# A literal engine order for the last attention and its mixture of experts, with both halves' expert tiles in one row

## The chip, the cores and the metric

The kernel runs on one core of one Trainium2 chip. The metric is the time of one execution in microseconds of the device. Times of before and after are medians over several runs. The profile is of one execution of its own.

## The reference

The input x holds 8 sequences of 256 tokens, 128 numbers each (2048 tokens in all); `ctx` is a context of 64 rows of 256 numbers for each sequence. Four levels L0 to L3 follow one another, each an attention to the context and a feed-forward part, added to x behind a gate:

```python
x = x + jnp.tanh(g_xattn[3]) * _L3_xattn_ref(ctx_2048, _layernorm(x, axis=-1), mask_BxS2_ik0, L3_xattn_b)
x = x + jnp.tanh(g_ffn[3]) * _L3_ffn_ref(_layernorm(x, axis=-1), L3_ffn_shared_w1, ...)
```

L3's attention has 8 heads of depth 16: `softmax(Q K^T / 4 + b - 1e30 (1 - mask)) V`, with K and V the two halves of the context. L3's feed-forward part is a mixture of experts:

```python
sw1, sw2 = (_bit_quant(shared_w1), _bit_quant(shared_w2))
shared_out = jax.nn.silu(jnp.einsum('btd,fd->btf', h, sw1)) @ sw2.T
probs = jax.nn.softmax(h @ router_w.T, axis=-1)
top_prob, top_idx = jnp.max(probs, axis=-1), jnp.argmax(probs, axis=-1)
h1 = jax.nn.silu(jnp.einsum('btd,efd->ebtf', h, ew1))
eo = jnp.einsum('ebtf,edf->ebtd', h1, ew2)
gate = jax.nn.one_hot(top_idx, N_EXPERTS) * top_prob[..., None]
return shared_out + jnp.einsum('ebtd,bte->btd', eo, gate)
```

Here `h` is a normalised x, the hidden width is 256, and of eight experts each token uses the most probable one.

## The kernel before, in words

x stays on the chip as 16 tiles of 128 tokens (`NT`), 4 chunks of 4 tiles (`NCH`, `TPC`), two halves of 8 tiles (`HT`). The stages run one after another: `l0`, `l1_xattn`, `l1_ffn`, `l2_xattn`, `l2_ffn`, `l3_xattn`, `l3_ffn`. The program says what each engine does, and a scheduler places the instructions of each engine in an order of its own, from its estimates of cost and the order of the program; `issue_after` (in `behind`) keeps an instruction behind a named one. Buffers come from pools with a fixed number of copies; a new tile waits until the old one's last reader is done. PSUM is eight single banks in both L3 stages.

**Attention, `l3_xattn` (L1760 to L1857).** For each of 16 tiles, `weights(t)` makes one score matmul against all heads and context rows at once (`sc`, 128x512, L1786), adds the mask on DVE (L1794), takes the maximum by head on DVE (`all_max`, L289), subtracts it on POOL (L1797), takes the exponential on ACT (L1798) and the sum on DVE (`row_sum`, L318). `turned(t)` transposes the probabilities on PE (`tp`, L1808) and copies them out on ACT (L1809). For each pair of tiles, `summed(b)` multiplies by the values (`o`, L1815), copies (L1817), transposes back (`po`, L1820), divides by the sums (L1822, L1824) and adds to x (L1831). The loop calls `weights` three tiles ahead. Into it are woven: `turn_weights` in the first ten steps (transposes of the expert weights, L1772, and an ACT copy, L1774); `normed3(c)` for chunks 1 to 3 at steps 0, 4 and 8 (layer norm by `ln_apply`, four DVE operations, and a transpose; chunk 0's stands ahead of the last `experts(3)` of `l2_ffn`); `logits3(c)` for chunks 0 to 2 at steps 4, 8 and 12 (norm by DVE statistics and `norm_act`, that is one DVE operation at L358 and four ACT operations at L360; a copy z to DRAM, a transpose, a matmul with the router weights); `routed3(0)` at step 9 and the gathers of half 0 from step 10.

**Routing, `routed3` (L1931).** From the logits of a half: softmax (L320 to L329), `largest` (L646), `counted` (L514, matmuls that count tokens by expert) and `placed` (L529), some 35 small DVE operations. They give each token a place in tiles that hold one expert's tokens each: 15 tiles a half. `sources` (L597) makes the list of tokens by 16 index matmuls (`dp_idx`, L602) and a cast (L604). `fetched3` gathers the 15 tiles of z by indirect DMAs that POOL issues (`gather`, L610).

**Mixture, `l3_ffn` (L1957).** `tiles(half, aside)` is a row of 15 tiles with four operations on each, one behind another by a step: `turn` (transpose L1972, ACT L1974), `first` (expert matmul, 256 wide, L1979, Silu on ACT L1987), `turn_back` (transposes L1992, DVE copy L1994), `second` (two matmuls L1999, DVE copy L2008; after every fourth tile SP writes four to DRAM, L2011). The expert's number is read by PE's sequencer (`tile_expert`). `aside` puts logits of chunk 3 and routing of half 1 in nine pieces into the row of half 0, and the gathers of half 1 at its step 10. `combine` (L623) gathers a half's results back, 8 gathers, and adds them times the probability to x (L640, DVE). `wide` and `shared` are the shared expert on a chunk (L2029 to L2036), with `add_back_t` (a copy on ACT and DVE in turn, L69 to L75, transposes L285, an addition L277). Order: row of half 0, its combination, dense chunk 0, row of half 1 (half 0's additions at steps 8 and 12), combination of half 1, dense chunks 1 to 3, additions of half 1, output (L2062, SP).

Of the kernel before, what the change touches and what calls it, by code (L numbers as in the profile page):

```python
# [24 lines left out]
P = 128  # L25
# [3 lines left out]
NCH = 4  # L29
# [8 lines left out]
def tile_flamingo(ctx: ExitStack, tc: tile.TileContext, a: dict, out: bass.AP, n_sub: int = 8):  # L38
# [1495 lines left out]
    def l2_ffn():  # L1534
        wqp, wkp, wvp, wop, w1p, w2p = (w2f[:, i] for i in range(6))
        load3()
        with psum(8, 0), tc.tile_pool(name="l2f", bufs=1) as cp, tc.tile_pool(name="l2g", bufs=2) as lp:
# [215 lines left out]
            normed3(0)  # L1753
# [3 lines left out]
    def normed3(c):  # L1757
        s.activation(q3["qT"][c % 2], transposed(layernorm(c)), AF.Copy, scale=0.25)

    def l3_xattn():  # L1760
# [15 lines left out]
        with psum(8, 0), tc.tile_pool(name="l3x", bufs=2) as lp:  # L1776
            madd, kb, qTs = q3["madd"], q3["kb"], q3["qT"]
            pTs, sums = {}, {}

            def weights(t):  # L1780

                b = t // 2
                if t % 2 == 0:
                    sums[b] = mk(small, [P, 2, 8], "rs3")
                sc = bank([P, 8, S2], "sc3")
                pe.matmul(  # L1786
                    sc.rearrange("p h m -> p (h m)"),
                    qTs[(t // TPC) % 2][:, (t % TPC) * P : (t % TPC + 1) * P],
                    kb[:, b].rearrange("p h m -> p (h m)"),
                    start=True,  # L1790
                    stop=True,
                )
                pa = mk(lp, [P, 8, S2], "pa3", bufs=4)
                v.tensor_tensor(pa, sc, under(madd[:, b, :], 8), ALU.add)  # L1794
                m = mk(small, [P, 8], "m3")
                all_max(m, pa)
                q3["sub"] = g.tensor_tensor(pa, pa, over(m, S2), ALU.subtract)  # L1797
                s.activation(pa, pa, AF.Exp)  # L1798
                row_sum(sums[b][:, t % 2, :], pa)
                return pa  # L1800

            def turned(t, pa):
                b = t // 2
                if t % 2 == 0:
                    pTs[b] = mk(lp, [P, 4, S], "pT3")
                tp = bank([P, 4, P], "tp")
                for i in range(4):
                    pe.transpose(tp[:, i, :], pa[:, 2 * i : 2 * i + 2, :].rearrange("p t m -> p (t m)"), ident)  # L1808
                s.copy(pTs[b][:, :, (t % 2) * P : (t % 2 + 1) * P], tp)  # L1809

            def summed(b):
# [4 lines left out]
                oT = mk(lp, [P, S], "oT3")  # L1816
                s.copy(oT, o)  # L1817
                po = bank([P, 2, D], "po3")
                for qt in range(2):
                    pe.transpose(po[:, qt, :], oT[:, qt * P : (qt + 1) * P], ident)  # L1820
# [11 lines left out]

            ahead = 3
            ready = {t: weights(t) for t in range(ahead)}
            for t in range(NT):
                if t % TPC == 0 and t // TPC + 1 < NCH:
                    normed3(t // TPC + 1)
                if t + ahead < NT:
                    ready[t + ahead] = weights(t + ahead)
                turned(t, ready.pop(t))  # L1840
                if t % 2:
                    summed(t // 2)
                if turns:
                    turn_weights(*turns.pop(0))

                if t in (4, 8, 12):
                    logits3(t // 4 - 1)
                elif t == 9:
                    run_all(routed3(0))
                elif t == 10:  # L1850
                    fetches = fetched3(0, 2)
                if t in (10, 11):
                    with behind(q3["sub"]):
                        next(fetches)
                elif t == 12:
                    with behind(q3["sub"]):
                        run_all(fetches)  # L1857
# [50 lines left out]
    def logits3(c):  # L1908

        st = mk(small, [P, TPC, 6], "st")  # L1910
        mv = mk(small, [P, TPC, 2], "mv")
        for k in range(TPC):
            v.bn_stats(st[:, k, :], xs(c)[:, k, :])
            v.bn_aggr(mv[:, k, :], st[:, k, :])
        rstd = mk(small, [P, TPC], "rstd")
        v.tensor_scalar(rstd, mv[:, :, 1], 1.0 + 1e-5, 1e-10, ALU.mult, ALU.add)
        power(rstd, rstd, TPC)
        z = mk(act, [P, TPC, D], "xn")
        norm_act(z, c, mv, rstd)
        half, k2 = divmod(c, 2)  # L1920
        if k2 == 0:
            q3["z", half] = dram.tile([HT * P, D], F32, tag=f"z{half}", name=f"z{half}")
        nc.sync.dma_start(q3["z", half][k2 * CW : (k2 + 1) * CW, :].rearrange("(n p) d -> p n d", p=P), z)
        hT = q3["hT"]
        s.activation(hT[:, c, :], transposed(z), AF.Identity, bias=gb3[:, 1:2], scale=gb3[:, 0:1])
        lg = bank([P, TPC, E], "lg")
        for k in range(TPC):
            pe.matmul(lg[:, k, :], hT[:, c, k * P : (k + 1) * P], rw3, start=True, stop=True)
        s.copy(q3["lg"][:, (c % 2) * TPC : (c % 2 + 1) * TPC, :], lg)

    def routed3(half):  # L1931


        pool = q3["pool"]
        pr = softmax8(q3["lg"])
        yield
        ((m, mask),) = largest(pool, pr, 1)
        w = mk(pool, [P, HT], "w3")
        v.tensor_scalar(w, m, tg[:, 7:8], None, ALU.mult)
        q3["w", half] = w  # L1940
        yield
        cnt = counted(pool, [mask])
        yield
        q3["at", half] = yield from placed(pool, [mask], cnt, q3["consts"])

    def fetched3(half, n=2 * HT):

        at, ge = q3["at", half][0:2]
        idx = sources(q3["pool"], at, ge)
        q3["xr", half] = xr = mk(q3["pool"], [P, idx.shape[1], D], "xr")  # L1950
        for t in range(idx.shape[1]):
            if t and t % n == 0:
                yield
            gather(xr[:, t, :], q3["z", half][:, :], idx[:, t : t + 1])

    def l3_ffn():


        with psum(8, 0), tc.tile_pool(name="l3f", bufs=3) as lp:
            w1T, w2T = q3["wT"]  # L1960
            w1e, w2e = (w.rearrange("p (e i) d -> p e i d", i=2) for w in (w1T, w2T))
            hT = q3["hT"]

            def tiles(half, aside):
                ei, xr = q3["at", half][2], q3["xr", half]
                n_tiles = xr.shape[1]
                yg = dram.tile([n_tiles * P, D], F32, tag=f"y3{half}", name=f"y3{half}")
                xrT, h1s, hTs, es, yr, marks = {}, {}, {}, {}, {}, {}

                def turn(t):  # L1970
                    pt = bank([P, P], "ptr")
                    pe.transpose(pt, xr[:, t, :], ident)  # L1972
                    xrT[t] = mk(lp, [P, P], "xrT")
                    s.activation(xrT[t], pt, AF.Identity, bias=gb3[:, 1:2], scale=gb3[:, 0:1])  # L1974

                def first(t):
                    es[t] = e = tile_expert(ei, t)
                    ph = bank([P, 2 * P], "phr")
                    pe.matmul(  # L1979
                        ph,  # L1980
                        xrT[t],
                        w1e[:, bass.ds(e + 1, 1)].rearrange("p e i d -> p (e i d)"),
                        start=True,
                        stop=True,
                    )
                    h1s[t] = mk(lp, [P, 2, P], "h1r")
                    marks[t] = [s.activation(h1s[t].rearrange("p i f -> p (i f)"), ph, AF.Silu)]  # L1987

                def turn_back(t):
                    pt = bank([P, 2, P], "pth")  # L1990
                    for i in range(2):
                        pe.transpose(pt[:, i, :], h1s[t][:, i, :], ident)  # L1992
                    hTs[t] = mk(lp, [P, 2, P], "h1T", bufs=2)
                    v.tensor_copy(hTs[t], pt)  # L1994

                def second(t):
                    y = bank([P, D], "yr")
                    for i in range(2):
                        pe.matmul(  # L1999
                            y,  # L2000
                            hTs[t][:, i, :],
                            w2e[:, bass.ds(es[t] + 1, 1), i, :].rearrange("p e d -> p (e d)"),
                            start=(i == 0),
                            stop=(i == 1),
                        )
                    if t % 4 == 0:
                        yr[t // 4] = mk(lp, [P, 4, D], "yr", bufs=2)
                    marks[t].append(v.tensor_copy(yr[t // 4][:, t % 4, :], y))  # L2008
                    if t % 4 == 3 or t == n_tiles - 1:
                        o, n = t - t % 4, t % 4 + 1  # L2010
                        nc.sync.dma_start(  # L2011
                            yg[o * P : (o + n) * P, :].rearrange("(n p) d -> p n d", p=P), yr[t // 4][:, 0:n, :]
                        )

                for t in range(-2, n_tiles + 1):
                    for f, d in ((turn, 2), (first, 1), (turn_back, 0), (second, -1)):
                        if 0 <= t + d < n_tiles:
                            f(t + d)
                    for f in aside.get(t, ()):
                        with behind(*marks.get(t - 1, ())):  # L2020
                            f()
                return yg
# [114 lines left out]
```

## Time and profile before

| | |
|---|---|
| median of 11 runs | 1323.03 us (1307.28 to 1331.52) |
| profiled execution | 1318.24 us, span 1316.3 us |
| mean granted TensorE clock | 0.866 |
| busy: PE | 1086.7 us (83%) |
| busy: DVE | 644.5 us (49%) |
| busy: ACT | 437.1 us (33%) |
| busy: POOL | 303.8 us (23%) |

The time of a profiled execution is its span and some 2 us around it. The stages of the end, from the timeline: L3's attention 1110.1 to 1215.6 us, row of half 0 to 1251.9, dense chunk 0 and row of half 1 to 1296.6, the rest to 1316.3. A page of the profile has the busy time of each engine (PE matmul, PEld weight load, DVE vector, ACT scalar, POOL, SP for DMA issue), its share by fortieths of the span, groups of instructions by line, and the timeline of one engine. In a group's row the columns are: line, engine, operation, output and input with their shapes, count; busy time and mean ns of one; idle time of the engine just ahead of them and what ended it. "remote" and "issue" name waits that ended for no reason which the profile shows.

### The profile page before, as it was taken

The numbers are of one execution on the slowest core, as the hardware profiler recorded it, in microseconds if no ns is written. First come the engines' busy times: TensorE is split into PE (matmuls) and PEld (weight loads), VectorE is DVE, ScalarE is ACT, GpSimd is POOL, SyncE is SP. The second block draws the span as 40 slices with busy tenths as digits, with TensorE's granted clock in tenths as the row PEclk, the third lists the DMA queues.
The fourth block names the chain that finished last, engine by engine and source line by source line (L and its number), as shares of the span: only waits on it lengthen the run. The fifth ranks groups of instructions, "written<-read, shape, count | busy, mean of one in ns | idle before, by whom it ended". The sixth has DMA issues, their size and how long they took to land.

```text
span 1316.3 us, 15627 instructions
## 1 busy us (share of the span) xinstructions
PE 1086.7 (83%) x5570; PEld 603.7 (46%) x5570; DVE 644.5 (49%) x1794; ACT 437.1 (33%) x842; POOL 303.8 (23%) x341
## 2 busy tenths in 40 slices
PE   6886697966999999899898987889988898655857
PEld 4554455643444444533455654344443333433734
DVE  4651333543655455443237986257518445653514
ACT  4521242322334433541234444211123333422523
POOL 2157221140100000100102554023133101215152
PEclk9887698975999979787898997988899999765869
DMA  9113110110000003200000002000000000002122
GB/s 246 39 31 53 34 45 22 33 52 8 19 14 7 18 2 98 97 0 0 1 1 1 1 1 59 22 0 1 1 0 0 1 0 0 9 8 38 37 48 79
DMA packets 50811, 37.04 MB, mean 28 GB/s; under 512 B 10280, under 2 KB 46672, under 8 KB 50480
## 3 DMA queue, kind: packets, MB, share of 16 engines
q1 hardware_dynamic: 45488, 26.83, 7.4%
q0 software_dynamic: 3968, 8.13, 3.1%
q10 hardware_dynamic: 1280, 1.09, 0.4%
q8 instruction: 45, 0.74, 0.2%
q14 instruction: 30, 0.25, 0.1%
HBM read 25.34 MB, written 8.13 MB: 25 GB/s over the span
## 4 chain that ended last, share of the span: by engine, by line
PE 65%; DVE 15%; ACT 7%; issue 6%; POOL 4%; another core or an unknown queue 2%; DMA 1%; SPq 1%; DVEq 0%; ACTq 0%; POOLq 0%
PE pymT L1610 4%; PE gur L768 4%; PE st L1038 4%; PE sc L983 4%; PE o L1064 3%; DVE nmx L992 3%; PE pqmT L1610 3%; PE phm L1693 2%; PE pgb L1591 2%; PE pvmT L1610 2%; PE pkmT L1610 2%; PE yr L793 2%; PE yt L1200 2%; PE gu L744 2%
## 5 line engine op out<-in xcount | busy, mean ns | idle before, releaser
L992 DVE TENSOR_REDUCE nmx<-sc 128x2 f32<-128x640 f32 x128 | 97.7, 817 | 80.3 <-PE sc L983 67.0
L221 POOL TENSOR_TENSOR rstd<-rstd,mhalf 128x4 f32<-128x4 f32 (+1 forms) x36 | 34.2, 950 | 383.2 <-DVE rstd L236 317.9
L1047 ACT ACTIVATE pT<-st 128x1024 f32<-128x1024 f32 x64 | 62.1, 1021 | 109.1 <-PE st L1038 109.1
L768 PE MATMUL gur<-arena_a,xrT 128*128 x184 | 70.0, 508 | 0.8 <-issue 0.4
L1610 PE MATMUL pymT<-xe,arena_b 128*128 128x512 f32 x128 | 61.7, 638 | 2.6 <-DVE xe L1602 2.6
L983 PE MATMUL sc<-arena_b 29*128 29x320 f32 x256 | 43.7, 571 | 15.1 <-DVE nmx L992 12.4
L610 POOL DMA_INDIRECT xr<-xk,dp_src x46 | 45.7, 994 | 43.1 <-DVE lg_m L289 29.4
L785 DVE COPY aTr<-pta 128x256 f32<-128x256 f32 x46 | 19.5, 423 | 73.1 <-PE pta L783 43.7
L1464 POOL TENSOR_TENSOR arena_a<-arena_a,rs 128x1024 f32<-128x1024 f32 x16 | 30.4, 1901 | 92.7 <-DVE rs L1463 78.7
L610 POOL DMA_INDIRECT xn<-yg,dp_rows x32 | 30.3, 946 | 75.4 <-DMA yg<-yr 43.1
L1591 PE MATMUL pgb<-gt,e_sel 8*128 8x512 f32 x192 | 40.4, 704 | 7.6 <-ACT gt L1584 7.6
L783 PE MATMUL pta<-ident,sgr 128*128 128x128 f32 x138 | 24.7, 291 | 22.4 <-issue 17.6
L1610 PEld LDWEIGHTS pymT<-xe,arena_b 128*128 128x128 f32 x128 | 25.5, 205 | 38.6 <-issue 23.7
L768 PEld LDWEIGHTS gur<-arena_a,xrT 128*128 128x128 f32 x184 | 35.0, 210 | 17.3 <-issue 7.7
L793 PE MATMUL yr<-arena_a,aTr 128*128 (+1 forms) x276 | 41.7, 292 | 0.0
L983 PE MATMUL sc<-arena_a 29*128 29x320 f32 x256 | 37.2, 492 | 4.1 <-DVE nmx L992 3.8
L610 POOL DMA_INDIRECT xr<-z,dp_src x30 | 28.7, 956 | 44.5 <-DVE dp_ef L318 27.8
L776 ACT ACTIVATE sgr<-gur 128x352 f32<-128x352 f32 x46 | 21.4, 464 | 52.3 <-PE gur L768 35.2
L1443 PE MATMUL sc<-G,t2k 128*128 128x512 f32 x64 | 34.3, 632 | 4.6 <-DVE rs L1462 3.7
L793 PEld LDWEIGHTS yr<-arena_a,aTr 128*128 128x128 f32 (+1 forms) x276 | 37.8, 207 | 0.2
L1038 PE MATMUL st<-arena_b 32*128 32x256 f32 x256 | 36.8, 502 | 1.2 <-DVE nmx L992 1.0
L277 DVE SCALAR_TENSOR_TENSOR x<-yt,tg,x 128x512 f32<-128x512 f32 x16 | 12.0, 748 | 52.2 <-PE yt L1205 29.1
(501 smaller groups left out, 2428.7 us busy)
## 6 DMA issues: line engine op xcount, KB each, us to landing
arena_a<-in_L_ffn_exp_wgu_dram SPq DMA_DIRECT2D x2, 1408.0 KB
yg<-yr SPq DMA_DIRECT2D x10, 256.0 KB
arena_a<-in_L_xattn_Wkv_dram SPq DMA_DIRECT2D x1, 2048.0 KB
y<-yr SPq DMA_DIRECT2D x6, 256.0 KB
x<-in_x_dram SPq DMA_DIRECT2D x4, 256.0 KB
arena_b<-in_ctx_dram ACTq DMA_DIRECT2D x2, 512.0 KB
arena_a<-in_L_ffn_exp_wd_dram SPq DMA_DIRECT2D x2, 512.0 KB
xk<-xk SPq DMA_DIRECT2D x4, 256.0 KB
```

Of the source, the lines that this page charges most:

```text
L221: g.tensor_tensor(dst, src, mhalf[:, 0:n], ALU.pow)
L610: return g.indirect_dma_start(out=dst, out_offset=None, in_=src, in_offset=bass.IndirectOffsetOnAxis(ap=idx, axis=0))
L768: pe.matmul(gu[:, h, 0:352], xrT[t], wgu[:, bass.ds(e + 1, 1), h * 352 : h * 352 + 352].rearrange("p e f -> p (e f)"), start=True, stop=True,)
L793: pe.matmul(y, aT[0:n, i, :], wd[0:n, bass.ds(e + 1, 1), i, :].rearrange("p e d -> p (e d)"), start=(i == 0), stop=(i == 2),)
L983: pe.matmul(scs[j // 2][:, j % 2, 0:K], qp[i : i + 29, k4, t], kp[i : i + 29, k4, b, :], start=True, stop=True,)
L992: l1["max"] = v.tensor_reduce(nmx[qt][:, h0 : h0 + 2], scs[pr][:, :, 0:K], AX.X, ALU.max, negate=True)
L1038: pe.matmul(sts[j // 2][:, j % 2, kt, :], kp[i : i + 32, k4, b, kt * P : (kt + 1) * P], qp[i : i + 32, k4, tb], start=True, stop=True,)
L1047: s.activation(pT[k4, pr], sts[pr], AF.Exp)
L1064: pe.matmul(o[kk][32 * i : 32 * i + n, k, :], w, e, start=(step == 0), stop=(step == 2))
L1443: pe.matmul(sc[:, 8 * k : 8 * k + 8, :].rearrange("p h m -> p (h m)"), xT[:, q], G[:, b, 8 * k : 8 * k + 8, :].rearrange("p h m -> p (h m) ...
L1591: pe.matmul(pg, e_sel4[r, e, :], gt[r], start=True, stop=True)
L1610: pe.matmul(pq, w[:, e, :], xe[:, e, :], start=(e == 0), stop=(e == E - 1))
```

## The change

Both L3 stages run under `manual_schedule` for PE, DVE, ACT and POOL: these engines take their instructions in the order of the program (SP is still scheduled). So the program's own order is written anew.

```diff
-            normed3(0)
+            for c in range(2):
+                for f in normed3(c):
+                    f()
             experts(3)
...
-        with psum(8, 0), tc.tile_pool(name="l3x", bufs=2) as lp:
+        with psum(8, 0), tc.tile_pool(name="l3x", bufs=2) as lp, tc.manual_schedule(engines=all_four):
...
+            beside(3, *normed3(2))
+            beside(7, *normed3(3))
+            for c in range(2):
+                beside(4 * c + 5, *logits3(c))
+            steps = routed3(0)
+            beside(12, *[lambda: next(steps, None)] * 5)
+            beside(13, *logits3(2))
+            scores(0)
+            scores(1)
+            shifted(0)
+            exps(0)
+            for t in range(NT + 1):
+                b = t // 2 - 1
+                if t % 2 == 0 and b >= 0:
+                    outputs(b)
+                if t + 2 < NT:
+                    scores(t + 2)
+                if t + 1 < NT:
+                    shifted(t + 1)
+                if t < NT:
+                    summed(t)
+                    turned(t)
+                if t % 2 == 0 and b >= 0:
+                    added(b)
+                if t + 1 < NT:
+                    exps(t + 1)
                 if turns:
                     turn_weights(*turns.pop(0))
...
+                for f in extra.get(t, ()):
+                    f()
```

`scores`, `shifted` (add, maximum, subtraction), `exps`, `summed` (now the sum by row), `turned`, `outputs` (value matmuls and copy) and `added` (transposes back, division, addition to x) are the pieces of the former `weights`, `turned` and `summed`. `normed3` and `logits3` become three steps each (statistics; normalisation, by `norm_act` in both; transposes and what follows), and `routed3` five, which now also makes the list of tokens; the softmax there takes its maximum from `largest`, and only the largest probability is computed (two DVE operations fewer). `fetched3(half, tiles)` only gathers.

```diff
+            stats, norm, logits = logits3(3)
+            fetched3(0, range(2))
+            stats()
+            h0, h1 = wide(0), wide(1)
+            norm()
+            fetched3(0, range(2, n_tiles))
+            y0 = shared(0, h0)
+            y1 = shared(1, h1)
+            logits()
+            back(0, y0)
+            back(1, y1)
             steps = routed3(1)
...
+            aside = {t: [lambda: next(steps, None)] for t in range(-1, 4)}
+            aside[4] = [lambda: fetched3(1, range(n_tiles))]
+            mid, backs = {}, []
+            aside[n_tiles - 4] = [lambda: mid.update(h=wide(2))]
+            aside[n_tiles - 3] = [lambda: mid.update(y=shared(2, mid["h"]))]
+            aside[n_tiles - 2] = [lambda: back(2, mid["y"])]
+            aside[n_tiles] = [lambda: backs.extend(combined(0))]
+            for i in range(2):
+                aside[2 * n_tiles - 4 + 2 * i] = [lambda i=i: backs[i]()]
+            for t in range(-2, 2 * n_tiles + 1):
+                for f, d in ((turn, 2), (first, 1), (turn_back, 0), (second, -1)):
+                    if 0 <= t + d < 2 * n_tiles:
+                        f(t + d)
+                for f in aside.get(t, ()):
+                    f()
+            h3 = wide(3)
+            tail = combined(1)
+            y3 = shared(3, h3)
+            back(3, y3)
+            for f in tail:
                 f()
```

So all gathers of half 0 are in the mixture, ahead of and beside dense chunks 0 and 1; the 30 tiles of both halves form one row (`n_tiles` is 15), with routing of half 1 in its steps -1 to 3, half 1's gathers at 4, dense chunk 2 at 11 to 13, half 0's combination at 15 and its additions at 26 and 28; dense chunk 3 and half 1's combination follow. `shared` no longer calls `add_back_t`: it copies on ACT always, and `back` does the transposes and the addition.

## The prediction

> **What bounds the kernel now.** The change touches only the L3 stages, so I first read the page's table by fortieths of the span (32.9 us each): PE is busy nine tenths in the middle and falls off at the end.
>
> ```profile
> PE   6886697966999999899898987889988898655857
> PEclk9887698975999979787898997988899999765869
> ```
>
> The last seven slices (from about 1086 us) hold PE at 5 to 8 tenths and the granted clock down to 5 tenths. Next come the windows by stage (columns: start and end, length, busy time of each engine with its instructions, clock, DMA share): the L3 attention in five parts, four parts of the tile row, the tail.
>
> ```profile
> 1109.40:1132.00 22.60, 16.27 (x82) 9.43 (x82) 19.36 (x44) 12.22 (x22) 7.68 (x10) 0.92 0.00 1
> 1132.00:1148.00 16.00, 10.69 (x36) 6.24 (x37) 6.09 (x22) 5.31 (x11) 4.05 (x4) 0.60 0.05 16
> 1148.00:1163.00 15.00, 8.60 (x53) 5.83 (x51) 8.70 (x23) 8.25 (x16) 4.13 (x4) 0.96 0.06 17
> 1163.00:1185.00 22.00, 12.78 (x48) 8.48 (x48) 13.53 (x52) 3.52 (x8) 2.14 (x2) 0.50 0.00 1
> 1185.00:1216.00 31.00, 17.13 (x68) 9.19 (x68) 9.26 (x24) 7.80 (x16) 17.51 (x18) 0.50 0.23 40
> 1216.00:1246.00 30.00, 24.92 (x135) 20.76 (x134) 15.11 (x66) 16.58 (x36) 1.07 (x2) 0.76 0.09 27
> 1257.00:1278.00 21.00, 7.43 (x24) 3.87 (x22) 1.18 (x2) 2.87 (x7) 13.33 (x15) 0.60 0.27 48
> 1278.00:1296.30 18.30, 17.13 (x114) 15.38 (x114) 11.46 (x36) 8.82 (x23) 0.00 (x0) 0.89 0.20 59
> 1296.30:1316.30 20.00, 12.24 (x36) 5.22 (x34) 6.11 (x14) 4.17 (x7) 7.61 (x8) 0.91 0.26 75
> ```
>
> The attention takes 106 us while no engine works more than 65.5 of them (PE), much of that at half clock; DVE works 56.9. It is bound by the order: an engine waits for one whose next instruction is something else. The groups by line show the idle time before each:
>
> ```profile
> L1797 POOL TENSOR_TENSOR pa<-pa,m 128x512 f32<-128x512 f32 x16 | 16.7, 1045 | 47.0 <-ACT pT L1809 15.9 <-DVE dp_gt L543 7.8 <-DVE sm_m L328 7.7
> L1794 DVE TENSOR_TENSOR pa<-sc,arena_a 128x512 f32<-128x512 f32 x16 | 10.9, 687 | 12.1 <-PE sc L1786 12.0
> L1809 ACT COPY pT<-tp 128x512 f32<-128x512 f32 x16 | 9.3, 584 | 35.0 <-PE tp L1808 30.7 <-remote 3.6 <-issue 0.8
> ```
>
> POOL's subtractions wait 15.5 us for routing on DVE and 15.9 for buffers that a late copy holds. The tile row has another loss: in 1257 to 1278 POOL issues gathers without a break and all else stalls. The timeline (start, duration, instruction, idle time before it):
>
> ```profile
> 1269.99 0.42 DVE L1994 COPY h1T<-pth 128x256 f32<-128x256 f32 x1 [11.91 <-remote]
> 1273.55 0.46 ACT L1974 ACTIVATE xrT<-ptr,gb 128x128 f32<-128x128 f32 x1 [6.67 <-issue]
> 1273.64 0.95 POOL L610 DMA_INDIRECT xn<-y,dp_rows  x1 [0.31 <-issue]
> ```
>
> Each hop between engines takes 3 to 12 us here though its producer is done; the Silus of one row step (L1987), 1.21 us apart when undisturbed, are 3.5 and 10.5 apart. The last line is the burst's last gather; from 1278 the row runs again.
>
> **The change, attention.** Work per engine stays nearly the same; each engine gets a literal order, two tiles apart on PE and one on DVE, and routing of half 0 is cut into five steps. DVE's rows: add .687, maximum .679, sum .680 for 16 tiles, 32.7 us; reciprocal .246, multiply .424, add to x .476 for 8 pairs, 9.2; five sets of statistics (chunks 2 and 3 of the queries, 0 to 2 of the mixture) at 2.1, 10.6; routing, some 35 operations of .21 and one of 1.22, 8.5. Sum 61.0. Row durations overlap a little: of about 62 us of rows the windows hold 56.9, so I take 0.92 of 61.0, 56. How tight will DVE be? The nearest pipeline of the same shape in this trace is the L2 attention:
>
> ```profile
> 712.00:784.00 72.00, 66.79 (x311) 42.84 (x309) 64.19 (x155) 33.30 (x71) 39.34 (x41) 1.00 0.00 1
> ```
>
> DVE is busy 89% there (87% with its head), PE at full clock. I take 87%: 64.5 us. The first scores come at 1110.8 (1110.15 before, and .65 of PE for the four transposes of normed3(1), moved into the L2 end; its statistics and normalisation lie beside experts(2)), add 1.1 to the first DVE work, and 6 for what stands alone at the end: the count matmuls' wait (1.2), the last output chain (1), the index matmuls (2 to 3.6) and a cast. Routing runs at steps 12 to 16, so index of half 0 and attention end together: **1182.4**, against 1185.1 for the index before but 1215.6 for the attention. normed3's normalisation goes from DVE to ACT: 4 x .317 of DVE against .163 and 4 x .48 of ACT, which has room (36.7 of 106 us busy). A subtraction on POOL is 1.05 and an Exp .63; with three hops of .1 these 2.0 us fit beside the 2.05 DVE us of a step, so one tile ahead just suffices.
>
> **Mixture, from that index.** (1) Dense chunks 0 and 1 and logits3(3) go ahead of the row: a dense chunk is 1.8 + 1.88 + .66 = 4.4 us of PE (rows of the tail), two of them and .9 of logits 9.7, and some 4.4 of hops: 14.1. Beside it POOL issues half 0's 15 gathers at 1.25 us (.95 and .30), 18.8; they end near 1204 while the row starts at 1196.5 and needs one per 1.21 us, so gathers hide, which before stood alone in 1185 to 1216. (2) The row: 30 x 1.21 = 36.3, and 2.1 to fill; 13 for routing of half 1 inside it (before, half 0's 14 steps beside routing and logits3(3) took 30.1 against 16.9, 13.2 more; half 1 has two DVE operations fewer, but no logits); 4.4 of dense chunk 2; and slow hops. For those the ends are nothing and what bursts cost before: 17 (1257 to 1278, 23 gathers), about 18 (L0, 23 in a row), 7 (L0, 16), 4 to 5 (half 0, 11 in a row), 1.5 (tail, 8). New bursts in the row are 13 (its end: I take 5), 15 (8.5) and 8 (2): 15.5, nearest to the bursts of like length. Row sum 71.3, from 1196.5 to 1267.8. (3) The tail is as before: the last tile's copy ended at 1296.6, the span at 1316.3, 19.7. Writing y, 8 gathers and the last additions are unchanged, and dense chunk 3 (4.4) lies beside the gathers, of which 9.7 us remain if it is late; half 0's combination (8 gathers at step 15, additions at 26 and 28) lies in the row. SP's output writes and y writes keep their order: no y write is queued behind an x that waits. POOL's order is literal as well: 13 gathers stand behind chunk 3's pow, half 0's combination behind 15 gathers, half 1's behind both, each ready before POOL is.
>
> Sum: 1182.4 + 14.1 + 71.3 + 19.7 = **1287.5**, 28.8 less than the span of 1316.3. The profiled execution took 1318.24 (1.9 around its span), 4.8 below the median of 1323.0; the same difference from the median gives **1294**.
>
> **The rivals.** *B, slow hops do not return* (-15.5): nothing but the rows above speaks for a price by burst, and the order of after leaves engines fewer hops to wait for. 1278; with DVE at 95% in the attention another 5.5, 1273. [...]
>
> *C, PE stays at half clock through the attention.* In windows of 4 us the clock fell to .68 behind one with PE 41% busy and to .50 behind one with 20% (1132 to 1136), and stayed at .50 in 1163 to 1216 at 55% busy. At half clock a step of PE costs 4.1 us (scores 1.71, probabilities' transposes .85, weight transposes .85 in ten of the steps, outputs .54 and .22), with logits and queries 76 in all: index at 1111.9 + 76 + 11.6 = 1199.5, 1304.6 in all, **1311**. Against it: at full clock PE needs 2.05 of the 4 us a step that DVE needs, about what held .92 to .96 above. [...]
>
> *D, slower: one tile ahead is too little and the literal order serialises a step.* Then a step is add .69, maximum .68, subtraction 1.05, Exp .63, transposes .85, copy .58 and six hops of .1, 5.1; 16 of them 82, and 20 for statistics and routing that no longer hide, 10 at head and index: index at 1223.5, **1335**. It decides from an index later than 1211 (1316.3 - 105.1), a step of over 4.6 us beside the rest. For it: before, three tiles ahead, a step took 6.6. Against: those steps waited for routing, not for the chain, and L2's attention at two ahead holds DVE at 87%.
>
> *E, no change*: gains are given back in waits for expert weights or buffers, 1323.
>
> **How the numbers follow.** Forecast .50, B .18, C .13, D .15, E .04. The predicted time is the forecast's, 1294. The range reaches from 1268 (B with the tighter DVE, and 5 less of routing in the row) to 1322 (all of C, most of E), leaving out D and a little more. A measurement of this kernel can tell about 0.5%, 6.6 us. Faster by more (under 1316.4): forecast, B and .09 of C, .77; within: the rest of C and most of E, .07; slower: D and a trace of E, .16.
>
> **What would show it.** In the profile after: DVE at 85% or more from the first score to the last index, which comes near 1182; POOL's subtractions no longer waiting for DVE's routing; half 0's gathers beside dense chunks; a row of 30 tiles at 1.21 us with gaps beside gather bursts of 8 to 15 us in all; a tail of 19 to 20. A granted clock of .5 in the attention would be C, steps over 4.6 us D, a row without gaps B. The prediction is wrong altogether if the stages before L3 move, since it takes them as unchanged.

## The result, and the profile after

The changed kernel takes 1300.46 us (median of 10 runs, 1293.35 to 1304.67) against 1319.9 of the kernel before in the same comparison (37 runs): ratio 0.9856, 95% interval 0.9831 to 0.9882, some 19 us less. Forecast were 29 less, 1294 us; the measured time lies in the range (1268 to 1322), which is wide. Its profiled execution took 1297.9 us, with a span of 1295.9, 20.4 less than before.

One thing is needed to read the numbers below: in two of the four sets of experiments (the first, of one run per kernel, and the third) the kernel before took 1254 to 1257 us, in the others 1322 to 1326, about as in the comparison above. I call these the lower and the upper level. So times are compared within a set. Between sets I compare what proved stable: stages counted from the first score matmul of L3 (L1786 before, L1801 after). In all executions with the attention as the change has it, at both levels, the first list of tokens was ready 76.4 or 76.5 us after it. The undisturbed distance of two steps of the tile row (from one Silu to the next) is 1.21 us. A hop is the handing over of a result from one engine to the next one; a slow hop is one where the next engine starts late.

By the page (busy tenths and granted clock in 40 slices) the last six slices are a little fuller than before (39 tenths in all against 36), and the clock is higher in four of the six:

```profile
PE   5886687976999999898898987889998999776775
PEclk9888698975999999887798997888999999986787
```

The windows of the changed kernel, cut where the forecast's terms end: attention in two parts, dense chunks ahead of the row, the row in five, the tail (start and end, length, busy time of PE, PEld, DVE, ACT and POOL with their instructions, clock, DMA share, GB/s):

```profile
1106.70:1153.00 46.30, 35.23 (x188) 20.16 (x188) 39.29 (x100) 29.70 (x62) 18.89 (x21) 0.95 0.04 12
1153.00:1183.20 30.20, 18.92 (x90) 12.82 (x89) 17.90 (x70) 7.96 (x18) 3.27 (x4) 0.61 0.03 9
1183.20:1196.60 13.40, 12.45 (x37) 6.41 (x38) 0.39 (x3) 7.02 (x13) 10.49 (x11) 0.77 0.25 61
1196.60:1216.00 19.40, 14.35 (x62) 10.52 (x60) 11.62 (x46) 7.37 (x15) 4.93 (x6) 0.65 0.20 23
1216.00:1240.00 24.00, 12.98 (x65) 9.35 (x64) 4.82 (x14) 5.78 (x15) 14.17 (x15) 0.73 0.38 64
1240.00:1254.50 14.50, 14.50 (x79) 10.89 (x78) 5.77 (x15) 6.94 (x18) 0.00 (x0) 0.86 0.10 32
1254.50:1267.80 13.30, 9.50 (x54) 7.35 (x53) 4.13 (x12) 4.65 (x12) 7.58 (x8) 0.87 0.21 61
1277.90:1295.90 18.00, 3.85 (x12) 1.33 (x10) 3.59 (x9) 1.78 (x3) 7.56 (x8) 0.69 0.27 76
```

For 46 us DVE is busy 85% (39.29), near the 87% taken from L2; in the last 30 us of the attention 59%, at a clock of 0.61. In the row, both of these stretches with POOL's gathers (1216 to 1240, 1254.5 to 1267.8) leave PE idle (busy 12.98 of 24.00 and 9.50 of 13.30 us), and the stretch between them without a gather has PE busy throughout (14.50 of 14.50).

In the first of them DVE and ACT start late though PE, their producer, is done; the timeline (start, duration, instruction, idle time before it):

```profile
1222.42 0.61 PE L2048 MATMUL yr<-bq_w,h1T 128*128 x4
...
1222.87 0.27 PE L2022 MATMUL ptr<-ident,xr 128*128 128x128 f32 x1
...
1225.16 0.70 PE L2031 MATMUL phr<-bq_w,xrT 128*128 x2 [2.03 <-issue]
...
1230.93 0.29 DVE L2051 COPY yr<-yr 128x128 f32<-128x128 f32 x1 [3.81 <-remote]
...
1232.40 0.46 ACT L2024 ACTIVATE xrT<-ptr,gb 128x128 f32<-128x128 f32 x1 [6.01 <-remote]
...
1232.91 1.22 PE L2031 MATMUL phr<-bq_w,xrT 128*128 x2 [4.30 <-issue]
...
1235.83 0.38 ACT L2033 ACTIVATE h1r<-phr 128x256 f32<-128x256 f32 x1 [2.97 <-remote]
1236.27 0.69 PE L2039 MATMUL pth<-ident,h1r 128*128 128x128 f32 x2 [2.14 <-ACT h1r L2033]
```

The three operations of DVE and ACT read what the first three lines of PE made, done at 1223.03, 1223.14 and 1225.86, and the two engines had been free for 3.81, 6.01 and 2.97 us. PE is not late: its two lower lines start .05 and .06 us after the operation of ACT just above them ends. Over all 30 tiles of the row, in the seven profiles of the upper level (before, changed twice, four variants), DVE and ACT start up to 8.2 us late behind PE, and PE never more than .14 us late behind them; in the four profiles of the lower level that keep gathers by POOL in the row, no hop of the row is more than .4 us late. The profile models the ends of matmuls, so it does not tell whether PE's result or the start of the next engine is what comes late.

The subtractions of the attention no longer wait for routing or for a late copy's buffers, but mostly (23.6 of 31.1 us) for the maximum just ahead of them (group by line, idle time and its releasers last):

```profile
L1814 POOL TENSOR_TENSOR pa<-pa,m 128x512 f32<-128x512 f32 x16 | 16.7, 1044 | 31.1 <-DVE m L289 23.6 <-PE pt L272 7.4
```

From the first score the terms compare thus (us):

| | before | forecast | after |
|---|---|---|---|
| list of tokens of half 0 ready | 75.0 | 71.6 | 76.4 |
| attention's last addition to x | 105.9 | 71.6 | 74.0 |
| from the list to the row's first transpose | (30.4) | 14.1 | 13.4 |
| row, to its last DVE copy (before with dense chunk 0, after with 2) | 81.0 | 71.3 | 81.3 |
| from there to the end | 19.7 | 19.7 | 18.0 |
| first score to end | 206.1 | 176.7 | 189.2 |

L3 became 17.0 us shorter; the other 3.4 of the profiles' difference lie ahead of L3's first score, where the change only adds a chunk's norm and transposes. Six executions of the changed program and its variants at this level have their first score anywhere from 1106.7 to 1124.4.

### The profile page after: what moved, and what is told of

Same layout as the page of the kernel before. It is cut to its first block, busy times and chain, and to the rows that moved or that the text cites. A ratio compares the mean times of both kernels' runs of the same rounds, so it can differ in the third digit from the quotient of the medians.

```text
span 1295.9 us, 15651 instructions
## 1 busy us (share of the span) xinstructions
PE 1076.7 (83%) x5570; PEld 595.9 (46%) x5570; DVE 641.0 (49%) x1776; ACT 443.0 (34%) x860; POOL 305.2 (24%) x341
## 4 chain that ended last, share of the span: by engine, by line
PE 62%; DVE 15%; ACT 6%; issue 5%; another core or an unknown queue 4%; POOL 4%; DMA 3%; SPq 1%; POOLq 0%; DVEq 0%; ACTq 0%
PE pymT L1610 5%; PE sc L983 4%; PE st L1038 4%; PE o L1064 3%; PE gur L768 3%; DVE nmx L992 3%; PE pqmT L1610 3%; PE phm L1693 2%; PE pgb L1591 2%; PE pvmT L1610 2%; PE pkmT L1610 2%; PE yr L793 2%; PE yt L1200 2%; PE gu L744 1%
## 5 line engine op out<-in xcount | busy, mean ns | idle before, releaser
L610 POOL DMA_INDIRECT xn<-yg,dp_rows x32 | 30.4, 951 | 74.9 <-DMA yg<-yr 42.4
L768 PEld LDWEIGHTS gur<-arena_a,xrT 128*128 128x128 f32 x184 | 34.8, 208 | 19.2 <-issue 9.5
L1038 PE MATMUL st<-arena_b 32*128 32x256 f32 x256 | 34.2, 461 | 1.3 <-DVE nmx L992 1.0
```

The costliest lines, as they stand in the source:

```text
L610: return g.indirect_dma_start(out=dst, out_offset=None, in_=src, in_offset=bass.IndirectOffsetOnAxis(ap=idx, axis=0))
L768: pe.matmul(gu[:, h, 0:352], xrT[t], wgu[:, bass.ds(e + 1, 1), h * 352 : h * 352 + 352].rearrange("p e f -> p (e f)"), start=True, stop=True,)
L1038: pe.matmul(sts[j // 2][:, j % 2, kt, :], kp[i : i + 32, k4, b, kt * P : (kt + 1) * P], qp[i : i + 32, k4, tb], start=True, stop=True,)
```

## The experiments

The first four, one run each, take half 1's gathers as the suspect of the slow steps in 1216 to 1240.

**Gathers left out.** Edit: the line that calls them in step 4 goes, and tiles read half 0's rows.

```diff
-                pe.transpose(pt, q3["xr", half][:, k, :], ident)
+                pe.transpose(pt, q3["xr", 0][:, k, :], ident)
...
-            aside[4] = [lambda: fetched3(1, range(n_tiles))]
```

> Left out: the 15 gathers of half 1; the row's tiles 15 to 29 read half 0's gathered rows instead, all else is as in the changed kernel. In the changed kernel six steps of the row beside these gathers take 21.5 us (Silu starts 1218.58 to 1240.05) where undisturbed steps of 1.21 would take 7.3. If the gathers slow each hop between engines (theory), the steps after routing stay at 1.21 until dense chunk 2 and the span falls by 12 to 14 us. If those steps are slow for another reason (the clock, expert numbers, buffers), they stay slow and the span falls by less than 3.

Measured: every step from the end of routing to dense chunk 2 is 1.20 to 1.21 us, the row 51.7 and not 81.3, the span from the first score 164.0. But the kernel before took 1257.29 in this set, and the same steps are undisturbed with gathers too (below). So it does not price the gathers.

**Arithmetic on POOL instead** (tiles again read half 0's rows).

```diff
-            aside[4] = [lambda: fetched3(1, range(n_tiles))]
+            def arith():
+                for t in range(n_tiles):
+                    g.tensor_tensor(q3["qT"][t % 2], hT[:, t % 2, :], hT[:, 0, :], ALU.subtract)
...
+            aside[4] = [arith]
```

> Left out: the 15 gathers of half 1, as in the kernel without them; in their place POOL does 15 subtractions of 128x512 (1.05 us each in the attention), so POOL is as busy, with no DMA. [...] If it is the gathers as such, steps are 1.21 and the span is that of the kernel without gathers, within 2 us.

Measured: the span from the first score is 183.6. Steps are 1.21 but for one of 24.74 (without gathers 5.96 there). The subtractions need no list of tokens and so ran early, in routing, and one small DVE operation lasted as long as they did, 16.99 us beside 16.55. The timeline (start, duration, instruction):

```profile
1166.17 16.99 DVE L551 SCALAR_TENSOR_TENSOR dp_end<-dp_pad,dp_base 128x8 f32<-128x8 f32 x1
1166.58 16.55 POOL L2099 TENSOR_TENSOR arena_a<-xT 128x512 f32<-128x512 f32 x15
```

DVE's operation takes .17 us in the changed kernel's trace. It lasted so long once in this run, and what made it do so was not shown. Beside the gathers the changed kernel's trace has another picture: DVE's operations keep their length (.41 to .43 for all 30 copies of L2041) and only start late (up to 6.0 us).

**Half the rows, and plain transfers** (in both, tiles read half 0's rows; the plain transfers stand at step 5).

```diff
-            aside[4] = [lambda: fetched3(1, range(n_tiles))]
+            def halves():
+                for t in range(n_tiles):
+                    gather(q3["xr", 1][0:64, t, :], q3["z", 1][:, :], q3["idx", 1][0:64, t : t + 1])
...
+            aside[4] = [halves]
```

> Changed: half 1's 15 gathers fetch 64 of 128 rows each, and tiles 15 to 29 read half 0's rows, so half the descriptors and half the bytes are moved. If the price follows descriptors or bytes (theory), the excess over 1.21 a step falls from 14 us to 4 to 8. If it follows the number of gather instructions and POOL's time for them, the excess stays at 12 to 15.

```diff
-            aside[4] = [lambda: fetched3(1, range(n_tiles))]
+            def plain():
+                for t in range(n_tiles):
+                    k = t % HT
+                    nc.sync.dma_start(q3["xr", 1][:, t, :], q3["z", 1][k * P : (k + 1) * P, :])
...
+            aside[5] = [plain]
```

> Changed: in place of half 1's 15 indirect gathers SP issues 15 plain DMAs of 128 rows of the same size (other rows), and tiles 15 to 29 read half 0's rows. The same bytes are written to the same buffer, in packets of 512 bytes. If DMA traffic to the buffer slows the hops (rival), the steps beside them stay slow by the share of bytes, 5 us or more in all. If it is what POOL does for an indirect gather (theory), steps stay at 1.21 and the span is that of the kernel without gathers, within 2 us.

Measured: steps of 1.21 in both (one of 1.33), rows of 51.8 and 51.7 us, spans from the first score 159.7 and 164.0. In the kernel with half rows the 8 gathers of half 0's combination are whole, and steps beside them are 1.20 and 1.21 too. So in this set nothing was slow, and both runs say nothing on descriptors or bytes. For the plain transfers the theory's steps of 1.21 came, but they decide nothing where nothing is slow at all.

The next set has the changed kernel and three variants of it.

> The changed kernel itself on the chip of this call, as a baseline beside the kernel before. If the slow hops beside gathers are the program's (theory), they return here as in the profile after: six steps of 21 us beside half 1's gathers, and a ratio to before near 0.986. If they belong to the chip (rival, raised by the 1.21 us steps beside half-size gathers), a chip with a time before near 1257 shows steps of 1.21 beside full gathers, and a ratio lower than 0.986, some 0.975.

Measured: 1308.44 us against 1321.71, ratio 0.9908 (0.9864 to 0.9951), and slow hops: the steps beside half 1's gathers are 3.68, 9.26 and 4.73. The span from the first score is 189.3, against 189.2 in the first profile.

**The scheduler's order in the attention.**

```diff
-        with psum(8, 0), tc.tile_pool(name="l3x", bufs=2) as lp, tc.manual_schedule(engines=all_four):
+        with psum(8, 0), tc.tile_pool(name="l3x", bufs=2) as lp:
```

> Undone: the literal order of the attention alone; the program is the changed one, but the scheduler orders PE, DVE, ACT and POOL there; the mixture keeps its literal order. If the attention's gain comes from the literal order (theory), half 0's index comes later by 5 us or more after the first score, and the time rises by 5 to 15 us against the changed kernel. If the new program order (five single steps of routing, no gathers) does it, the scheduler finds about the same order and the time is within 4.

Measured: neither theory holds, since the scheduler's order is the better one. List of tokens at 65.2 (11.2 earlier than under the literal order), last addition at 65.6 (8.4 earlier), span from the first score 180.2, that is 9.1 less; 1296.99 us, ratio to before 0.9836 (0.9771 to 0.9900). The trace names the idle time of DVE ahead of the division (L1849), first the changed kernel, then this one (releaser: us, times):

```profile
  PE po L1845: 14.4, 5
```

```profile
  PE po L1845: 3.9, 1
```

Under the literal order DVE stands before a division whose operand PE has yet to transpose, five times. In the longest of these waits (6.02 us, to 1158.82) the logits that routing reads had been copied by 1154.75, but routing's first operation (L289 of `largest`) stands behind the division and started at 1159.68. The clock differs too: from 40 to 50 us after the first score it was 0.75 under the literal order and 1.00 under the scheduler's. Whether that is a cause of the later end or an effect of the waits was not separated.

**The scheduler's order in the mixture.** The same edit at `l3f`.

> Undone: the literal order of the mixture alone; the program is the changed one, but the scheduler orders the four engines there. If the row of 30 tiles needs the literal order (theory), routing of half 1 or a combination's additions get ahead of tiles on DVE and the row takes 5 to 15 us more. If the row's order in the program is enough, the time is within 4 of the changed kernel.

Measured: 1308.83, ratio 0.9895 (0.9837 to 0.9954); span from the first score 187.7, 1.6 less; row 80.0 against 81.4. The order in the program is enough.

**Dense chunks 2 and 3 beside half 1's gathers.**

```diff
-            aside[n_tiles - 4] = [lambda: mid.update(h=wide(2))]
-            aside[n_tiles - 3] = [lambda: mid.update(y=shared(2, mid["h"]))]
-            aside[n_tiles - 2] = [lambda: back(2, mid["y"])]
+            aside[5] = [lambda: mid.update(h2=wide(2))]
+            aside[6] = [lambda: mid.update(h3=wide(3))]
+            aside[7] = [lambda: mid.update(y2=shared(2, mid["h2"]))]
+            aside[8] = [lambda: mid.update(y3=shared(3, mid["h3"]))]
+            aside[9] = [lambda: back(2, mid["y2"])]
+            aside[10] = [lambda: back(3, mid["y3"])]
...
-            h3 = wide(3)
...
-            y3 = shared(3, h3)
-            back(3, y3)
```

> Moved: dense chunk 2 from steps 11 to 13, and dense chunk 3 from behind the row, into steps 5 to 10, beside half 1's gathers. Where gathers slow the hops (theory), the longer matmuls fill the waits: the row with both chunks is 4 to 9 us shorter than the changed kernel's row and tail. Where hops are not slow, chunk 3's 4.4 us move from beside the last gathers into the row, and the time rises by 3 to 5.

Measured: 1303.64, ratio 0.9888 (0.9806 to 0.9969); row 78.5 with both chunks against 81.4 with one, tail 19.4 against 18.0: together 1.6 less, below the 4 to 9 expected. The steps that hold the dense chunks are still 4.14, 8.74 and 7.24: waits are filled only in part.

The third set is again one with a low time before (1254.36).

**The last piece of a pair one step later** (literal order).

```diff
-            for t in range(NT + 1):
+            for t in range(NT + 2):
...
-                if t % 2 == 0 and b >= 0:
+                if t % 2 == 1 and b >= 0:
                     added(b)
```

> Changed: in the literal order of the attention, the last piece of a pair (transposes back, division, addition to x) stands one step later than in the changed kernel; all else is the same. If the literal order loses because DVE waits in place for these transposes (theory: 14.4 us of idle time ahead of the division in the changed kernel, 3.9 with the scheduler's order), that idle time falls below 4, half 0's first gather comes 66 to 70 us after the first score and not 76.7, and the stage span from the first score falls from 189.3 to 179 to 183. If the loss is the clock or routing's place (rival), the index stays at 75 to 77.

Measured: DVE's wait ahead of the division is gone,

```profile
  PE po L1845: 0.7, 3
```

but the list of tokens comes at 72.7 (first gather 73.0, expected 66 to 70), and the last addition at 74.0 as before. PE's timeline at the end (last bracket: idle time and its releaser):

```profile
1117.38 1.12 PE L1830 MATMUL tp<-ident,pa 128*128 128x128 f32 x4 [5.58 <-ACT pa L1817]
1118.29 0.64 PE L1845 MATMUL po<-ident,oT 128*128 128x128 f32 x2
1120.16 1.63 PE L272 MATMUL pt<-ident,xn 128*128 128x128 f32 x4 [1.23 <-ACT xn L360]
1122.65 1.88 PE L1968 MATMUL lg<-L_ffn_router_w_t,xT 128*128 128x8 f32 x8 [0.87 <-ACT xT L1965]
1124.46 1.08 PE L1837 MATMUL o<-pT,vc 128*32 128x256 f32 x8
1125.47 3.60 PE L602 MATMUL dp_idx<-dp_ge,dp_at 128*128 128x15 f32 x16
1128.91 0.67 PE L1845 MATMUL po<-ident,oT 128*128 128x128 f32 x2
```

The last tile's transposes (`tp`) wait 5.58 for its exponential. The last pair's value matmul (`o`) stands behind the transposes and logits of chunk 2, which wait for ACT, and its `po` behind 3.6 us of index matmuls (clock 0.50 there). One wait in place was taken away, and the next ones in the queue set the end. The row starts 3.2 us earlier (86.6); 1223.87 us, ratio to before 0.9792 (0.9730 to 0.9855). In this set full gathers stand beside undisturbed steps; ACT's Silus, then POOL:

```profile
1164.48 0.38 ACT L2033 ACTIVATE h1r<-phr 128x256 f32<-128x256 f32 x1
...
1165.69 0.38 ACT L2033 ACTIVATE h1r<-phr 128x256 f32<-128x256 f32 x1
...
1166.89 0.38 ACT L2033 ACTIVATE h1r<-phr 128x256 f32<-128x256 f32 x1
```

```profile
1164.12 0.94 POOL L610 DMA_INDIRECT xr<-z,dp_src  x1 [0.30 <-issue]
1165.37 0.94 POOL L610 DMA_INDIRECT xr<-z,dp_src  x1 [0.30 <-issue]
```

This trace and that of the changed kernel run the same program up to L3, so they also show where the two levels part. From the first to the last of L0's 78 gathers the changed kernel takes 221.6 us (73.71 to 295.34) and this one 176.3 (76.71 to 252.99), 45.4 less. From there to L3's first score, 811 and 804 us without a gather, they differ by 7.8 only. From there to the end they differ by 32.9, and the row makes 29.7 of that. So most of what sets the levels apart lies in the stretches with gathers.

**Two edits together:** the scheduler's order in the attention, and both dense chunks in the row.

> Two edits that helped, together: the attention ordered by the scheduler, and dense chunks 2 and 3 beside half 1's gathers under the literal order. If their gains add up (9.1 and 1.6 us of the span from the first score), that span is 178 to 180, and the ratio to before 0.980 to 0.985. If the gathers' slow hops take it back, it is above 182.

Measured: 1220.42 against 1254.36, ratio 0.9748 (0.9704 to 0.9791), the lowest here and below the expected range, though its interval overlaps that of the later piece; against the changed kernel only the stage can be compared, 6.0 us less than the 159.7 of the changed kernel with half rows at this level. The list of tokens comes at 65.2 and the last addition at 65.6, as in the first kernel with this attention. The span expected belongs to the upper level and cannot be checked; it is 153.7 here, against 156.2 with the later piece in the same set. Row and tail, 57.2 and 19.2, are 6.7 longer than those of the later piece (51.6 and 18.0): where hops are not slow, chunk 3 loses its cover beside the last gathers, as the expectation of that move said, by more than its 3 to 5.

**Gathers in bunches**, each held back by a copy on POOL that reads the row's last result.

```diff
+            def ticked(t, f, *a):
+                half, k = divmod(t - 1, n_tiles)
+                g.tensor_copy(tick, yr[half][:, k % 4, 0:1])
+                f(*a)
...
+            aside[4] = [lambda: fetched3(1, range(5))]
+            aside[10] = [lambda: ticked(10, fetched3, 1, range(5, 10))]
+            aside[19] = [lambda: ticked(19, fetched3, 1, range(10, 15))]
...
+            aside[23] = [lambda: ticked(23, lambda: backs.append(next(at15)))]
```

> Changed: half 1's 15 gathers go in bunches of 5 at steps 4, 10 and 19 and half 0's combination in bunches of 4 at steps 15 and 23, each later bunch held back by a small copy on POOL that reads the row's last result; all else as in the changed kernel. If only long unbroken bursts slow the hops (theory of a backlog), the excess over 1.21 us a step beside gathers falls from some 21 us to under 8, and the span from the first score to 175 to 180. If each gather has its price, about 0.9 us (14.2 by 15), the excess stays at 17 to 22 and the span within 3 of 189. On a chip where hops are not slow, the span changes by under 2.

Measured: in this set nothing was slow, and bunches cost: one step of 5.65 us waits for a late bunch; row 59.6 and not 51.7, span 167.6. Expected was a span within 2 of the undisturbed one, which is 159.7 with half rows, so that failed. The ratio is 0.9874 (0.9810 to 0.9939). Whether bunches help where hops are slow stays open.

**Routing earlier.** The last kernel ran where the time before is 1325.83. It has the later last piece too; its further edit is:

```diff
-            beside(12, *[lambda: next(steps, None)] * 5)
+            for t in (12, 12, 13, 13, 14):
+                beside(t, lambda: next(steps, None))
```

> Changed: as in the kernel with the later last piece, and the five steps of routing half 0 stand in the attention's steps 12, 12, 13, 13 and 14, not 12 to 16. With the later piece alone the first gather came at 73.0 us after the first score, with DVE waiting 4.3 at the end for the index matmuls; with the scheduler's order at 65.5. If the pieces' places make that difference (theory), the first gather comes at 64 to 69 and the end-of-attention wait is gone, so the row's first Silu, which came at 88.2, comes at 82 to 86. If a literal order as such costs, because an engine cannot pass over a piece that waits (rival), the two more pieces in steps 12 and 13 wait for their count matmuls in place: the first gather comes at 71 or later and the first Silu stays at 87 to 90.

Measured: half of each. The first gather comes at 67.3, as the theory has it. But DVE now waits 2.9 in place for the count matmuls, as the rival has it, the last addition moves to 75.4, and the row starts at 87.3. (The first Silu came at 96.3; at this level the changed kernel has 95.6.) The span is 190.7: the list is 5.7 us earlier than with the later piece alone, and the row starts 0.7 later, since the attention's end stands ahead of the row in PE's order. 1307.19 us, ratio 0.9876 (0.9835 to 0.9916).

## Why the prediction was right, point by point

The direction was right, and the time falls in a range that reaches almost to the time before; of the 28.8 us forecast for the span, L3 gave 17.0. The total came as near as it did partly by luck. Against the forecast the list was 4.8 late, the way from it to the row 0.7 short, the row 10.0 too long and the tail 1.7 short; 4.1 of this was made good because L3 began at 1106.7 and not at 1110.8, though the prediction took the stages ahead of L3 as unchanged.

- **Attention.** The sign, DVE as the pacing engine and its work were right: 85% of the first 46 us at a clock of .95, and 57.2 us in all against 56. But over the 76.4 us to the list that is 75%, where 85% or more were forecast. The term "6 for what stands alone at the end" failed: the last 30 us ran at 59% of DVE. The list came 4.8 later than forecast, a little later than before; the attention's own end came 31.9 earlier than before. With two dense chunks put into the time won, the row starts 15.6 earlier, which is nearly all of L3's gain.
- **Literal order.** The forecast took it as what makes the pipeline. It costs time: the scheduler, given the changed program, has the list 11.2 us earlier and the attention's last addition 8.4 earlier. In the mixture the literal order made no gain either (1.6 us less without it). So what gains is the new program. Which part of it (routing in pieces at the end, gathers out of the attention, dense chunks beside them) gains how much was not tried one by one.
- **Dense chunks ahead of the row**: 13.4 against 14.1, with gathers hidden as worked out but for slow hops at the row's start (next point).
- **The row**: the failing size. Slow hops were priced at 15.5, worked out from bursts of like length. Against the undisturbed row of 51.6 (later last piece) the row lost 29.7, nearly twice that: 4.2 at its start (priced at 5), 15.4 in five steps beside half 1's gathers (21.5 us where 6.0 were due) and 2.0 in the next step (priced at 8.5), 7.9 in six steps beside and behind half 0's combination (priced at 2). The expectation of the first experiment counts those five steps as six and so has 14 for the excess. The undisturbed row is below the forecast's own 55.8 without slow hops: its first seven steps, beside routing, took 16.1 where 8.5 were due, so routing cost 7.6 and not 13. The two errors in part cancel. The 8 to 15 us of gaps that the forecast named as a sign were too low as well. Its reading of the hops was right in part: idle times of 3 to 12 us before DVE and ACT are there, but some of that is waiting for PE's work (of the 11.91 us, 5.9 lie behind the end of PE's transposes), and hops into PE are not slow.
- **The tail**: 18.0 against 19.7, with dense chunk 3 hidden.
- **B** (no slow hops) describes two sets of runs, but not with its time: there the kernel before takes 1254 to 1257. That it loses nothing by slow hops there either is likely, but no profile of it at that level was taken.
- **C** is seen only at the end: the clock is 1.00 for 30 us from the first score, .75 to .84 for the next 30, and .50 only from 60 us on. **D** did not happen for most of the attention: the first 13 exponentials start 3.4 us apart on average (1110.48 to 1151.29), not 5.1. The last three follow at 7.7, 4.7 and 5.2 us, beside routing and the waits told above.

What stays open: why hops beside gathers are slow in some sets of runs and not in others. The chip's number does not tell (the two levels occurred under the same number), and the program does not (same instructions). Length of the burst, descriptors and bytes could not be told apart, as the runs for it fell where nothing was slow. What makes DVE and ACT late behind PE, and PE never late behind them, was not found. Which single piece of the literal order costs the 11.2 us of the list was not found either: the two repairs each moved the wait to the next piece.

## What to carry to other kernels

Under a literal order small operands that came late became idle time of the whole engine here: DVE idled 14.4 us in five waits ahead of the division, 3.9 in one under the scheduler's order. So regroup the program first, compare the scheduler's order of it, and fix the order only where that wins. Follow the end of the stage and not one milestone: a list that was ready 9 us earlier started the row 2.5 us earlier and ended the kernel no sooner. Count a stage from its own first instruction, since its start moved by up to 17.7 us between executions, about as much as the change was worth. For a wait, compare its start with the end of the operation that it waits for: idle time alone made hops into PE look slow that were not.

## What the runs showed of the hardware

In the kernel with arithmetic on POOL, one 128x8 DVE operation lasted 16.99 us, from .41 us ahead of fifteen subtractions of 128x512 in a row on POOL (16.55 us) to .03 behind their end; the same operation takes .17 in the changed kernel. Beside the changed kernel's fifteen indirect gathers in a row on POOL the durations of DVE's and ACT's operations stayed the same (.42 and .29 for DVE's copies of L2041 and L2051, .46 and .38 for ACT's operations of L2024 and L2033). In some sets of runs their starts behind PE came up to 6.0 us late (changed kernel; 8.2 in the worst of seven profiles). Beside half 1's gathers the changed kernel has the first such start at 1220.26, in the fourth gather, and the last at 1237.40, 3.0 us behind the end of the fifteenth. PE's starts behind DVE and ACT were at most .14 late in all seven. In the other sets no hop of the row was more than .4 late beside the same gathers, and the kernel before as a whole took 1254 to 1257 us there and not 1322 to 1326.
